# Column-tiled channel sums in a one-core Mamba block: LayerNorm's mean and variance in three column tiles, x_proj in two

## The chip, the cores and the metric

The kernel runs on one core of a Trainium2 chip. The metric is the device time of one execution in microseconds. A core has a matrix engine (TensorE: PE for its products, PEld for its weight loads), a vector engine (VectorE, DVE), an activation engine (ScalarE, ACT), GpSimd (POOL), and a queue engine (SyncE, SP) that mostly issues DMAs. Each engine works through its own instructions in order; semaphores hold an instruction until its inputs are there.

## The reference

The input x has shape (8, 384, 32, 32): 8 images, 384 channels, 1024 tokens. Two layers are computed, each with a residual. The second is a mixture of four experts over the channels. The first is a Mamba block, and the change touches two places in it: the mean and variance over the channels of every token, and the small projection x_proj.

```python
x = x + _L0_conv_ref(_gn(x), ...)      # group norm, then the Mamba block
x = x + _L1_conv_ref(_gn(x), ...)      # group norm, then 4 experts

def _L0_conv_ref(x, ...):
    t = x.transpose(0, 2, 3, 1).reshape(b, L, c)
    mu = t.mean(-1, keepdims=True)
    var = t.var(-1, keepdims=True)
    t = (t - mu) * jax.lax.rsqrt(var + 1e-05) * ln_w + ln_b
    xz = t @ in_proj_w.T
    xm, z = jnp.split(xz, 2, axis=-1)
    xc = ...                             # causal convolution of 3 taps over xm, then silu
    dbc = xc @ x_proj_w.T                # 768 -> 24 + 16 + 16
    dt, Bm, Cm = jnp.split(dbc, [dt_rank, dt_rank + d_state], axis=-1)
    dt = jax.nn.softplus(dt @ dt_proj_w.T + dt_proj_b)
    ...                                  # scan over the tokens with 16 states per channel
    y = (ys + xc * D) * jax.nn.silu(z)
    t = y @ out_proj_w.T
    t = gelu(t @ mlp_w1.T + mlp_b1) @ mlp_w2.T + mlp_b2
    return t
```

## The kernel before

All data are f32. The tokens are cut into NCH = 16 chunks of T = 512 tokens, two per image. Channels lie on the 128 partitions, J = 3 to a partition; the 768 inner channels make ND = 6 blocks of 128 partitions. A product of 128 x 128 weights with 128 x 512 data fills one bank of PSUM.

The middle of the program is a loop of 384 rounds (line 922), 24 per chunk: one round is one block d of channels with one quarter s of the 16 states. In each round GpSimd forms the drive of the scan (L742), ScalarE the decays by exponentials (da_A and da_B, L734), VectorE runs four scans (L750) and half of the read-out (L754, the other half is GpSimd's), and in the round after, TensorE adds the states up by four products of 32 columns each, which stand side by side in the array (y, L776). Everything else is a list of tasks that is fed into the gaps of these rounds: the next chunk's normalization, in_proj, convolution, gate and x_proj; this chunk's dt; the previous chunk's out_proj and MLP; the gate and hidden layer of the experts. These are called fillers here. The second layer of the experts (L1026) is a stage of its own after the loop.

The order is written by a planner when the program is built. The program has three slots per round. A task is a generator that yields the engine it needs next, what it charges for it, and how many slots it wants to wait first. Each slot gives TensorE's account 2.7 (PE_SLOT, line 35), with at most 4 kept over; "bank" means TensorE and a free one of the four shared PSUM banks; a task is resumed where the account allows it, in order of rank and of time. plan(i, k) begins the tasks of round k of chunk i: the convolutions of the next chunk at k = 5 to 10, x_proj at k = 11, norm of the chunk after the next at k = 21, and, in every second chunk, the statistics of the next image at k = 3. The compiler doesn't reorder what the planner wrote (the block is under manual_schedule), and each engine follows it in order.

norm(i) (L257) takes a chunk's mean mu over the 384 channels with three full products into one bank (L265, weights mean_w: the mean over channels already scaled by the group norm), and VectorE subtracts it (L267). ScalarE squares the three parts (L274), with two buffers for them, and three full products sum the squares (L278, var). Then follow a logarithm and an exponential on ScalarE (L280, L281), VectorE's scaling (L283) and ScalarE's weight and bias (L287). All columns of the weights cmean and mean_w are equal, so that every partition of mu and var gets the sum. x_proj(i) (L350) is six products with 56 columns that accumulate in one bank (L358), and a copy by ScalarE into dbc (L363).

One place already works with column tiles: scores(b) forms the gate's logits with three products of 32 columns side by side (L573), copies the 96 partitions (L577, ScalarE), and adds the parts with small products (L580).

## Time and profile before

| what | us |
|---|---|
| median of 3 runs (4087.91 to 4099.21) | 4095.63 |
| the profiled execution | 4110.87 |
| its span, first to last instruction | 4109.0 |
| TensorE busy (share of the span) | 3709.2 (90%) |
| VectorE busy | 3032.3 (74%) |
| GpSimd busy | 2782.5 (68%) |
| ScalarE busy | 2422.7 (59%) |
| products of mu, L265: records, busy | 96, 49.3 |
| products of var, L278: records, busy | 96, 56.8 |
| products of x_proj, L358: records, busy | 192, 91.8 |

An f32 product is run in two passes and leaves two records, so 96 records are 48 products: three in each of 16 chunks. The busy time of a group is the union of its records; the end of a product is modelled, and products overlap in the record, so that the distance from one start to the next says more than a duration. Idle time named after a group of instructions is that of its engine just before them, with the instruction that ended it. The granted clock of TensorE was 0.948 of full speed over the span.

### The profile page before, as it was taken

How to read it: one execution, taken by the hardware profiler on the slowest of the kernel's cores; microseconds unless marked ns; L12 is line 12 of the kernel's file. 1: busy time of each engine (PE TensorE's matmuls, PEld its weight loads, DVE VectorE, ACT ScalarE, POOL GpSimd, SP SyncE). 2: the span in 40 equal slices, each digit the busy share in tenths (PEclk: the TensorE clock that was granted, in tenths of full speed). 3: DMA queues.
4: the chain of work that ended last, by engine and by line, in shares of the span. 5: the costliest groups of instructions: out<-in, count | busy, mean ns of one | idle time of the engine just before them, and what ended most of it. 6: DMA issues, size and time to landing. Idle time of an engine off the chain costs nothing. (4 is left out here: it accounts for less than half of the span.)

```text
span 4109.0 us, 35186 instructions
## 1 busy us (share of the span) xinstructions
PE 3709.2 (90%) x10294; PEld 1385.4 (34%) x10294; DVE 3032.3 (74%) x3081; ACT 2422.7 (59%) x3762; POOL 2782.5 (68%) x1070
## 2 busy tenths in 40 slices
PE   6678888999999999998999989898999899889999
PEld 2123223333333333333333333333333334334444
DVE  4888888878887878888878787878787781165552
ACT  4657676767686768676766677677767663200000
POOL 3898988788877888888878888888878881000000
PEclk8779898999999999999999999999999999899999
DMA  4444444464545454555455444555554543465552
GB/s 127 134 137 134 152 142 158 143 201 164 172 150 180 164 167 151 192 166 175 154 187 172 159 163 159 181 167 166 165 167 155 163 161 96 169 222 189 185 188 98
DMA packets 372499, 665.31 MB, mean 162 GB/s; under 512 B 40252, under 2 KB 151228, under 8 KB 370132
## 3 DMA queue, kind: packets, MB, share of 16 engines
q1 hardware_dynamic: 342352, 610.02, 45.8%
q10 hardware_dynamic: 29956, 53.05, 3.4%
q8 instruction: 83, 1.36, 0.1%
q14 instruction: 108, 0.88, 0.1%
HBM read 535.90 MB, written 127.01 MB: 161 GB/s over the span
## 5 line engine op out<-in xcount | busy, mean ns | idle before, releaser
L742 POOL TENSOR_TENSOR du<-dxr,b 128x2048 f32<-128x2048 f32 x384 | 1740.9, 4534 | 25.1 <-PE y L776 15.1
L754 POOL TENSOR_TENSOR du<-du,c 128x1024 f32<-128x1024 f32 x384 | 905.8, 2359 | 229.2 <-DVE du L750 199.7
L734 ACT ACTIVATE da_A<-dtr_a,w_a_log 128x512 f32<-128x512 f32 x768 | 527.6, 687 | 280.3 <-DVE du L754 122.1
L734 ACT ACTIVATE da_B<-dtr_b,w_a_log 128x512 f32<-128x512 f32 x768 | 527.3, 687 | 260.4 <-DVE du L750 207.2
L478 PE MATMUL hid<-tt,mlp_w 128*128 128x512 f32 x1152 | 541.5, 613 | 63.8 <-ACT h L482 46.7
L776 PE MATMUL y<-du,sel 128*32 128x512 f32 x3072 | 466.3, 642 | 134.1 <-DVE du L754 92.2
L750 DVE TENSOR_TENSOR_SCAN du<-da_B,carry,du 128x512 f32<-128x512 f32 x384 | 488.4, 1272 | 123.2 <-ACT da_B L734 114.8
L619 PE MATMUL e_hid<-xn,e_w 128*128 128x512 f32 x1080 | 519.2, 627 | 55.4 <-ACT r L623 37.9
L295 PE MATMUL g_in<-xt,in_proj 128*128 128x512 f32 x1152 | 554.7, 619 | 13.8 <-ACT xt L287 7.0
L517 PE MATMUL acc<-h,mlp_w 128*128 128x512 f32 x1152 | 543.4, 614 | 24.5 <-ACT h L493 15.9
L750 DVE TENSOR_TENSOR_SCAN du<-da_B,du 128x512 f32<-128x512 f32 x384 | 464.7, 1210 | 130.5 <-ACT da_B L734 114.0
L1026 PE MATMUL acc<-r,w_e_w 128*128 128x512 f32 x1152 | 496.6, 594 | 13.1 <-DVE r L1023 13.1
L750 DVE TENSOR_TENSOR_SCAN da_A<-da_A,carry,du 128x512 f32<-128x512 f32 x384 | 489.3, 1274 | 9.6 <-ACT da_A L734 9.0
L750 DVE TENSOR_TENSOR_SCAN da_A<-da_A,du 128x512 f32<-128x512 f32 x384 | 465.5, 1212 | 27.0 <-ACT da_A L734 25.0
L754 DVE TENSOR_TENSOR du<-da_A,c 128x1024 f32<-128x1024 f32 x384 | 470.3, 1225 | 13.2
L478 PEld LDWEIGHTS hid<-tt,mlp_w 128*128 128x128 f32 x1152 | 215.8, 193 | 366.5 <-issue 239.1
L517 PEld LDWEIGHTS acc<-h,mlp_w 128*128 128x128 f32 x1152 | 216.6, 195 | 343.9 <-issue 247.7
L295 PEld LDWEIGHTS g_in<-xt,in_proj 128*128 128x128 f32 x1152 | 210.0, 194 | 353.5 <-issue 255.1
L619 PEld LDWEIGHTS e_hid<-xn,e_w 128*128 128x128 f32 x1080 | 207.4, 199 | 356.2 <-issue 250.3
L1026 PEld LDWEIGHTS acc<-r,w_e_w 128*128 128x128 f32 x1152 | 219.6, 191 | 290.1 <-issue 287.3
L456 PE MATMUL g_out<-xc,out_proj 128*128 128x512 f32 x576 | 284.0, 641 | 32.9 <-DVE xc L783 32.9
L407 POOL TENSOR_TENSOR dtx<-dt,xc 128x512 f32<-128x512 f32 x96 | 122.1, 1272 | 217.5 <-DVE dt L404 217.5
(129 smaller groups left out, 3030.2 us busy)
## 6 DMA issues: line engine op xcount, KB each, us to landing
dxr<-dxr_dram SPq DMA_DIRECT2D x384, 256.0 KB, 4.7
mlp_w<-in_mlp_w SPq DMA_DIRECT2D x384, 192.0 KB, 2.9
dtr_b<-dtr_dram SPq DMA_DIRECT2D x192, 256.0 KB, 4.2
dtr_a<-dtr_dram SPq DMA_DIRECT2D x192, 256.0 KB, 3.2
r_dram<-r ACTq DMA_DIRECT2D x192, 256.0 KB, 3.5
r<-r_dram SPq DMA_DIRECT2D x64, 768.0 KB, 4.8
in_proj<-in_in_proj SPq DMA_DIRECT2D x192, 192.0 KB, 4.0
e_w<-in_e_w SPq DMA_DIRECT2D x192, 192.0 KB, 3.2
```

The costliest lines, as they stand in the source:

```text
L295: PE.matmul(g, lhsT=w[:, j, :], rhs=xt[i][:, j, :], start=(j == 0), stop=(j == J - 1))
L407: G.tensor_tensor(dtx, dt, xc[i, d], ALU.mult)
L456: PE.matmul(g, lhsT=w[:, d, :], rhs=xc[i, 3 * k + d], start=(k + d == 0), stop=(k == 1 and d == 2))
L478: PE.matmul(g, lhsT=w[:, j, :], rhs=tt[i][:, j, :], start=(j == 0), stop=(j == J - 1))
L517: PE.matmul(g, lhsT=w[:, n, :], rhs=hs[mine[n]], start=(k + n == 0), stop=(k == 1 and n == 2))
L619: PE.matmul(h, lhsT=w[:, j, :], rhs=xn[:, j, :], start=(j == 0), stop=(j == J - 1))
L734: S.activation(out, dtr[i, d][pair][:, j % 2, :], AF.Exp, scale=neg_a[:, d, j, s:s + 1])
L742: G.tensor_tensor(du[r], dxr[i, d], wide(bt[i, s].unsqueeze(1), [P, Q, T]), ALU.mult)
L750: V.tensor_tensor_scan(a if j < 2 else b, a, b, start, ALU.mult, ALU.add)
L754: engine.tensor_tensor(du[r][:, js, :], h, wide(ct[i, s].unsqueeze(1), [P, 2, T]), ALU.mult)
L776: PE.matmul(y[j * m:(j + 1) * m, :], lhsT=sel, rhs=h[:, j, :], start=False, stop=(s == NG - 1), tile_position=(0, j * m), skip_group_check ...
L1026: PE.matmul(acc[j], lhsT=e2[:, e, d, j, :], rhs=r[:, d, :], start=(e + d == 0), stop=(e + d == E + J - 2))
```

## The change

The mean, the variance and x_proj each get a new form. over_channels computes three products of 32 columns, side by side in the array, each into its own 32 partitions of the bank; ScalarE copies these 96 partitions into a buffer, and one full product with the constant matrix spread (1/32 everywhere) adds the three parts and writes the sum to all 128 partitions. x_proj takes its six blocks in three pairs: two products of 64 columns stand side by side, blocks 0, 2 and 4 accumulate in the lower half of the bank, 1, 3 and 5 in the upper half; ScalarE copies the bank, and one product with sum_x adds the halves. Its weights are padded to 64 columns for this, in a zeroed tile. The pool of the square buffers grows from two to three and also holds the copies, the loads of the statistics (which had a buffer of their own) and the skip matrix, which is used once. The planner's charges for these tasks change, and norm begins at k = 18.

```diff
--- before.py
+++ after.py
@@ -126,8 +126,8 @@
 
     wp, p1, p2 = pool("wp", 1), pool("p1", 1), pool("p2", 2)
     pxt, pdu, px1 = pool("pxt", NH), pool("pdu", 3), pool("px1", 2)
-    psq, pz, pxc, ph = pool("psq", 2), pool("pz", ND), pool("pxc", 2 * ND), pool("ph", HID)
-    pbc, pst, pxn, pr = pool("pbc", NG), pool("pst", 1), pool("pxn", 1), pool("pr", 2)
+    psq, pz, pxc, ph = pool("psq", 3), pool("pz", ND), pool("pxc", 2 * ND), pool("ph", HID)
+    pbc, pxn, pr = pool("pbc", NG), pool("pxn", 1), pool("pr", 2)
     pw_in, pw_out, pw_1, pw_2 = pool("pw_in", 3), pool("pw_out", 3), pool("pw_1", 3), pool("pw_2", 3)
     pw_e = pool("pw_e", 3)
     ps_a, ps_b, ps_y = pool("ps_a", 1, space=PSUM), pool("ps_b", 1, space=PSUM), pool("ps_y", 1, space=PSUM)
@@ -153,7 +153,12 @@
     ln_b = weight("ln_b", [P, J])
     conv_w = weight("conv_w", [P, ND, 3])
     conv_b = weight("conv_b", [P, ND])
-    w_x = weight("x_proj", [P, ND, DTR + 2 * NS])
+
+    w_x = wp.tile([P, ND, 64], F32, name="w_x_proj")
+    G.memset(w_x, 0.0)
+    S.dma_start(w_x[:, :, 0:DTR + 2 * NS], io["x_proj"])
+    sum_x = wp.tile([P, DTR + 2 * NS], F32, name="sum_x")
+    V.tensor_tensor(sum_x, ident[:, 0:DTR + 2 * NS], ident[:, 64:64 + DTR + 2 * NS], ALU.add)
     w_dt = weight("dt_proj", [DTR, DI])
     b_dt = weight("dt_b", [P, ND])
     neg_a = weight("a_log", [P, ND, Q, NG])
@@ -166,6 +171,9 @@
     S.dma_start(gate_w[:, :, 0:E], io["gate_w"])
     sum_j = wp.tile([32 * J, E], F32, name="sum_j")
     V.tensor_reduce(sum_j, ident[0:32 * J, 0:32 * J].rearrange("p (j m) -> p m j", j=J)[:, 0:E, :], AX.X, ALU.add)
+
+    spread = wp.tile([32 * J, P], F32, name="spread_j")
+    G.memset(spread, 1.0 / 32)
     e_b1 = weight("e_b1", [P, E * J])
     S.activation(neg_a, neg_a, AF.Exp)
     V.tensor_scalar(neg_a, neg_a, -1.0, None, ALU.mult)
@@ -177,8 +185,6 @@
 
     sel = wp.tile([P, P // Q], F32, name="sel")
     V.tensor_reduce(sel, ident.rearrange("p (m k) -> p m k", k=Q), AX.X, ALU.add)
-    skip = wp.tile([P, P], F32, name="skip")
-    V.tensor_scalar(skip, ident, d_skip[:, 0:1], None, ALU.mult)
 
     edge0 = wp.tile([P, ND, 2], F32, name="edge0")
     V.tensor_copy(edge0, wide(conv_b.unsqueeze(2), [P, ND, 2]))
@@ -236,7 +242,7 @@
                     part = xt[k][:, j, :]
                 else:
                     yield "-", 0, 3
-                    part = pst.tile([P, T], F32, name="part")
+                    part = psq.tile([P, T], F32, name="sq")
                     nc.sync.dma_start(part, chunk_of(io["x"], b * NH + k)[:, j, :])
                     yield "-", 0, 3
                 yield "DVE", 0.7, 0
@@ -248,34 +254,41 @@
         small = bank("shift")
         PE.matmul(small[:, 0:1], lhsT=cmean, rhs=g[:, 1:2], start=True, stop=True)
         yield "ACT", 0.6, 2
-        mean_w = p1.tile([P, P], F32, name="mean_w")
-        S.activation(mean_w, cmean, AF.Identity, scale=g[:, 0:1])
+        mean_w = p1.tile([P, 32], F32, name="mean_w")
+        S.activation(mean_w, cmean[:, 0:32], AF.Identity, scale=g[:, 0:1])
         S.activation(g[:, 1:2], small[:, 0:1], AF.Identity, bias=g[:, 1:2], scale=-float(J))
         free()
         gn[b] = g, mean_w
 
+    def over_channels(out, weights, parts):
+        for j in range(J):
+            PE.matmul(out[32 * j:32 * (j + 1), :], lhsT=weights, rhs=parts[j], start=True, stop=True,
+                      tile_position=(0, 32 * j))
+        yield "ACT", 0.6, 2
+        rows = psq.tile([P, T], F32, name="sq")[0:32 * J, :]
+        S.copy(rows, out[0:32 * J, :])
+        yield "PE", 1, 2
+        PE.matmul(out, lhsT=spread, rhs=rows, start=True, stop=True)
+
     def norm(i):
         while i // NH not in gn:
             yield "-", 0, 1
         g, mean_w = gn[i // NH]
         x = xt[i]
-        yield "bank", 3, 0
+        yield "bank", 1.2, 0
         mu = bank("mu")
-        for j in range(J):
-            PE.matmul(mu, lhsT=mean_w, rhs=x[:, j, :], start=(j == 0), stop=(j == J - 1))
+        yield from over_channels(mu, mean_w, [x[:, j, :] for j in range(J)])
         yield "DVE", 1.8, 2
         V.scalar_tensor_tensor(x, x, g[:, 0:1], wide(mu.unsqueeze(1), [P, J, T]), ALU.mult, ALU.subtract)
         free()
-        sq, var = [], None
-        for j in range(J + 1):
-            if j < J:
-                yield "ACT", 0.65, 2 * (j == 0)
-                sq.append(psq.tile([P, T], F32, name="sq"))
-                S.activation(sq[j], x[:, j, :], AF.Square, bias=g[:, 1:2])
-            if j > 0:
-                yield "PE" if var else "bank", 1, 1
-                var = var or bank("var")
-                PE.matmul(var, lhsT=cmean, rhs=sq[j - 1], start=(j == 1), stop=(j == J))
+        sq = []
+        for j in range(J):
+            yield "ACT", 0.65, 2 * (j == 0)
+            sq.append(psq.tile([P, T], F32, name="sq"))
+            S.activation(sq[j], x[:, j, :], AF.Square, bias=g[:, 1:2])
+        yield "bank", 1.2, 2
+        var = bank("var")
+        yield from over_channels(var, cmean[:, 0:32], sq)
         yield "ACT", 1.2, 2
         S.activation(var, var, AF.Ln, bias=eps)
         S.activation(var, var, AF.Exp, scale=-0.5)
@@ -348,14 +361,21 @@
         exp_ln_tables()
 
     def x_proj(i):
-        g = None
         m = DTR + 2 * NS
-        for d in range(ND):
-            while (i, d) not in xc:
+        for d in range(0, ND, 2):
+            while (i, d) not in xc or (i, d + 1) not in xc:
                 yield "-", 0, 1
-            yield "bank" if d == 0 else "PE", 1, 1 if d % 3 == 0 else 0
-            g = bank("g_x") if d == 0 else g
-            PE.matmul(g[0:m, :], lhsT=w_x[:, d, :], rhs=xc[i, d], start=(d == 0), stop=(d == ND - 1))
+            yield "bank" if d == 0 else "PE", 1.1, 1 if d != 2 else 0
+            if d == 0:
+                g = bank("g_x")
+            for k in range(2):
+                PE.matmul(g[64 * k:64 * (k + 1), :], lhsT=w_x[:, d + k, :], rhs=xc[i, d + k], start=(d == 0),
+                          stop=(d == ND - 2), tile_position=(0, 64 * k))
+        yield "ACT", 0.6, 2
+        halves = psq.tile([P, T], F32, name="sq")
+        S.copy(halves, g)
+        yield "PE", 1, 2
+        PE.matmul(g[0:m, :], lhsT=sum_x, rhs=halves, start=True, stop=True)
         yield "ACT", 0.6, 2
         while i > 0 and (i - 1, ND - 1) not in projected:
             yield "-", 0, 1
@@ -764,6 +784,8 @@
 
         y = yp[i, d] = ps_y.tile([P, T], F32, name="y")
         if i + d == 0:
+            skip = psq.tile([P, T], F32, name="sq")[:, 0:P]
+            V.tensor_scalar(skip, ident, d_skip[:, 0:1], None, ALU.mult)
             PE.matmul(y, lhsT=skip, rhs=xc[i, d], start=True, stop=True)
         else:
             S.activation(y, xc[i, d], AF.Identity, scale=d_skip[:, d:d + 1])
@@ -850,7 +872,7 @@
                 load_c(n, k - (per - NG) - 1)
         if k == 0 and i > 0:
             load_c(i, NG - 1)
-        if k == 21 and n + 1 < NCH:
+        if k == 18 and n + 1 < NCH:
             begin(norm(n + 1))
         if k == 3 and i + NH < NCH:
             begin(next_x(i))
```

## The prediction

> **What bounds the kernel now.** I read the page's busy shares first, then busy time by stretch, then groups by shape, then TensorE's timeline in single rounds, then the waits. Busy time by stretch (length; busy us and instruction count of PE, PEld, DVE, ACT, POOL; granted clock; DMA):
>
> ```profile
> 1000.00:2000.00 1000.00, 926.78 (x2710) 339.90 (x2709) 811.70 (x808) 710.72 (x1111) 824.06 (x314) 0.97 0.52 169
> 3600.00:4109.00 509.00, 496.61 (x1152) 219.59 (x1152) 268.32 (x304) 0.00 (x0) 0.00 (x0) 0.99 0.51 174
> ```
>
> In the scan loop (76 to about 3400 us) TensorE is 93% busy, VectorE 81%, GpSimd 82%, ScalarE 71%. TensorE is the first limit, but not by much. The closing stage holds no LayerNorm and no x_proj, so it stays as it is.
>
> TensorE's timeline over a few rounds gives the prices (start, duration, instruction; each f32 product leaves two records):
>
> ```profile
> 1944.97 1.12 PE L396 MATMUL g_dt<-dbc,w_dt_proj 24*128 24x512 f32 x2
> 1946.02 5.42 PE L456 MATMUL g_out<-xc,out_proj 128*128 128x512 f32 x12
> 1951.37 1.06 PE L776 MATMUL y<-du,sel 128*32 128x512 f32 x8
> 1952.37 2.84 PE L456 MATMUL g_out<-xc,out_proj 128*128 128x512 f32 x6
> ...
> 2140.44 3.06 PE L278 MATMUL var<-sq,cmean 128*128 128x512 f32 x6
> 2145.03 1.10 PE L776 MATMUL y<-du,sel 128*32 128x512 f32 x8 [1.53 <-DVE du L754]
> 2146.06 4.56 PE L456 MATMUL g_out<-xc,out_proj 128*128 128x512 f32 x10
> 2155.33 2.08 PE L456 MATMUL g_out<-xc,out_proj 128*128 128x512 f32 x2 [4.71 <-DVE xc L783]
> ```
>
> Starts count, not the modelled ends. Six products in a train take 1951.37 - 1946.02 = 5.35 us, **0.89 us** each; a group of four 32-column products takes 1952.37 - 1951.37 = **1.00 us**; a product alone between others (g_dt) **1.05 us**. The last four lines show a chunk border: the last round has only the three products of var, and TensorE then waits 1.53 and 4.71 us for VectorE.
>
> The waits between 1000 and 3000 us (waiting instruction, releaser: us, times, longest):
>
> ```profile
> DVE du L750 <- ACT da_B L734: 150.1, 145, 3.2
> DVE xc L314 <- ACT edge L312: 40.2, 20, 2.8
> DVE xc L314 <- ACT xc L308: 26.4, 20, 2.6
> ```
>
> VectorE in turn waits for ScalarE, most of all for the exponentials (da_B).
>
> The same stretch form, cut at the starts of y (chunk 8 is even, chunk 9 odd; the edges are rounds 0 to 21 and 22 to 23 of chunk 8, then 0 to 15, 16 to 22, 23 of chunk 9, and round 0 of chunk 10):
>
> ```profile
> 1723.80:1924.30 200.50, 185.83 (x530) 68.64 (x530) 161.81 (x176) 141.94 (x217) 165.51 (x74) 0.97 0.54 175
> 1924.30:1935.50 11.20, 8.30 (x31) 2.51 (x32) 11.10 (x14) 5.32 (x8) 10.36 (x6) 1.00 0.66 199
> 1935.50:2076.00 140.50, 129.59 (x400) 47.28 (x403) 118.26 (x109) 108.90 (x178) 118.54 (x38) 0.99 0.47 158
> 2076.00:2139.40 63.40, 61.46 (x175) 22.90 (x174) 47.07 (x43) 42.71 (x63) 48.09 (x17) 0.97 0.53 171
> 2139.40:2145.00 5.60, 4.11 (x15) 1.13 (x14) 5.57 (x6) 3.55 (x6) 5.17 (x3) 1.00 0.81 198
> 2145.00:2157.30 12.30, 7.56 (x20) 2.51 (x20) 9.77 (x11) 8.42 (x13) 9.39 (x5) 0.84 0.92 306
> ```
>
> The long stretches are TensorE's (93, 92 and 97%); the ends of chunks are VectorE's (11.10 of 11.20, 5.57 of 5.60). So a product removed in the long stretches gains time, one removed at the end of a chunk gains none.
>
> **What the Trainium skill says.** "TensorEngine Tiling (Array Packing)", Key Properties: tiles run in parallel, and changing the tiling mode drains the engine. The trace agrees in kind: the group of four takes 1.00 us instead of 4 x 0.89, about 0.1 over one product. "TensorE: Matmul & The Clock Gate", Measured speedup vs the span model, gives 2.38 times for three column tiles; the trace shows such triples only in L573, below. The same page, in "Architectural detail: the array is 16× 32×32, not 1× 128×128", has ScalarE's and VectorE's queues strictly in order, with only TensorE's weight loads pulled ahead. The waits agree: VectorE's order ends 92.2 of the 134.1 us that y's products wait in the whole run. So a late copy on ScalarE stops the product that reads it and all TensorE work behind.
>
> **The change part by part.** Groups by shape (busy, mean ns | idle before):
>
> ```profile
> L358 PE MATMUL g_x<-xc,w_x_proj 128*56 128x512 f32 x192 | 91.8, 611 | 4.2 <-ACT xc L346 4.2
> L278 PE MATMUL var<-sq,cmean 128*128 128x512 f32 x96 | 56.8, 719 | 12.0 <-ACT sq L274 12.0
> L573 PE MATMUL g_logits<-x,w_gate_w 128*32 128x512 f32 x96 | 24.0, 745 | 20.5 <-DVE dt L404 17.7 <-ACT x L569 2.7
> L580 PE MATMUL g_logits<-sum_j,x 96*128 96x4 f32 x128 | 17.0, 256 | 0.7 <-ACT x L577 0.7
> L577 ACT COPY x<-g_logits 96x512 f32<-96x512 f32 x16 | 9.1, 572 | 2.0 <-PE g_logits L573 2.0
> ```
>
> 1. *mu and var.* Each loses three products in a train (2.68 us) and gets one triple and one full product. The triple isn't shown in this place: at best it is one product, 0.89; at worst L573's 24.0 / 16 = 1.5, which includes a clock lowered by waiting. I take the group of four's 1.00. The adding product: 0.89 to 1.05; I take 1.05. Gain 0.63 each.
> 2. *x_proj.* Six products (5.35) become three pairs and one product. Pairs of 64 columns occur nowhere: 0.89 to 1.5, or, if they don't overlap, 1.78, which would undo the gain. I take 1.00. Gain 5.35 - 4.05 = 1.3.
> 3. So 2.56 us of TensorE per chunk. 15 chunks do this inside the loop (chunk 0's own is ahead of it): 38 us. Bounds from the ends above: 1.5 + 1.05 for mu and var is a gain of 0.1 each, with x_proj at 5.55 a loss of 0.2, together nothing; at 0.89 throughout one product is saved for mu, one for var and two for x_proj, 3.56 us a chunk, 53 us.
> 4. *Copies.* Three per chunk on ScalarE, 0.57 each from L577: 1.7 us per chunk on an engine that is 71% busy, hidden as long as the adding product stands far enough behind. In L573/L577/L580 the kernel has this very pattern, with L580 stopping TensorE for 0.7 us in 16 chunks. Against it, var waited 12.0 us for squares. Bounds per added wait: 0 to 0.75 (12.0 / 16).
> 5. *Buffers.* The third square buffer ends the squares' wait for var's products (10.3 us over the run), mostly beside other work: nothing. Loads of the statistics now rotate through the same three buffers; each buffer comes round two allocations later, longer than its reader needs, so SP's queue and the weight loads behind gain no wait; if one came, it would cost a DMA landing, 3.9 us.
> 6. *Set-up.* x_proj's weights are zeroed and loaded later, but first needed at 49.97 us; the small tiles fill idle time of POOL and VectorE. Before the loop the chain is serial: mu takes 5.2 us now for three slow products, then one triple, copy and product, -0.7; var +1.0; x_proj +1.8 (copy 0.57, product 1.05, handover). Net +2.1.
> 7. *Placement.* The order of both programs can be listed before either runs, and this decides most. The planner charges less for the tiles, so other products move forward. Filler products per round in a repeating pair of chunks (triple or pair as 1): even chunk, rounds 0 to 21: 174, then 173; rounds 22 to 23: 6, then 1. Odd chunk, rounds 0 to 15: 120, then 117; 16 to 22: 59, then 53; round 23: 3, then 10. So the even chunk loses its products where VectorE sets the time and gains about nothing. The odd chunk loses 9 x 0.89 = 8.0 us in TensorE's stretches, and gets 7 in round 23, 6.2 us, where 1.53 + 4.71 us of waiting stand free. Together -0.9 - 8.0, and +2.0 for ten groups at 0.11 over a product and six lone products at 0.16: -6.9 per pair.
> 8. *What comes back.* Six added waits per pair at 0.15: +0.9. The normalization of even chunks' successors ends later, so convolutions come two to a round in rounds 7 and 8 of odd chunks; VectorE's waits for their ScalarE part average (40.2 + 26.4) / 40 = 1.7 us, and I take part of one, +1.2 (bounds: 0, where the second stands ready meanwhile, and two waits, 3.4). Net -4.8 per pair.
>
> Chunks 3 to 14 are six pairs: -29. Chunks 0 to 2 aren't limited by TensorE (144 fillers in chunk 2 become 138, one of them outside its last two rounds): -1. Chunk 15 and all products after the loop stand as before: 0. With the set-up -28 us: 4110.9 (span 4109.0 plus 1.9 around it) becomes 4083, a ratio of 0.9932. The median of the runs shown lies 0.37% below the profiled execution; by the same ratio it becomes 4095.6 x 0.9932 = 4068.
>
> **The rivals.**
> *A, the whole gain:* neither waits nor convolutions cost anything and pairs overlap fully; 6 x -8.9 is -53, 4043. For it: 61.46 of 63.40 in rounds 16 to 22. Against it: VectorE is 74% busy there, and evens follow. 15%.
> *B, next limits:* rounds of 7 fillers take 7.25 us, and VectorE and GpSimd need about 7 (811.70 and 824.06 per 1000 us, 8.6 us per round); the freed time turns into waits between them, or the 64-column pairs run one after the other. -5, 4090. 20%.
> *C, slower:* the copies stand in ScalarE's order between exponentials of the scan and evictions, exactly where VectorE already waits 150.1 us for da_B. TensorE stops at the adding product, and the scan behind it. 45 such products in the loop; against a best gain of 53 this decides from 1.2 us each, against my sum from 0.15 + 28 / 45 = 0.77. At 1.3 us instead of 0.15: +52 - 28, 4119. For it: before hid TensorE waits up to 2.8 us for ScalarE's evictions (ACT h). Against it: L580's 0.7. 17%.
> *The forecast:* 48%, from 4050 to 4085.
>
> **How the numbers follow.** A measurement here tells 0.3%, 12 us, from no change. Faster: A, 43 of the forecast's 48, 6 of B: 64%. Same: 5, 12 of B, 2 of C: 19%. Slower: 2 of B, 15 of C: 17%. The range runs from beyond A's middle, 4037, to 4110, leaving out most of C.
>
> **What would show it.** Right: mu, var and g_x fall from 49.3, 56.8 and 91.8 busy us to some 33, 33 and 65; odd chunks get shorter and even ones hardly; the 4.71 us wait for xc goes at odd ends and grows at even ones. Wrong: adding products with more than 0.6 us idle before them, g_x near 102 (six products at 0.89 and one at 1.05 in 16 chunks), or VectorE's waits for da_B grown by tens of us.

## The result, and the profile after

The changed kernel takes 4114.54 us (median of 7 runs, 4108.00 to 4121.48) where the kernel before takes 4097.01 us in runs beside it. The ratio is **1.0043, 95% interval 1.0028 to 1.0058**: slower by 17.5 us, where 28 us less were forecast. The profiled execution took 4114.54 us, 3.7 us more than that of the kernel before (4110.87), which was longer than any of the seven runs behind that kernel's median (4087.91 to 4108.82). So the two traces show where time moved, and the medians how much was lost.

The page's head and the busy time by stretch of the changed kernel (length; busy us and instruction count of PE, PEld, DVE, ACT, POOL; granted clock; DMA share, GB/s):

```profile
span 4112.8 us, 35416 instructions
PE 3686.0 (90%) x10390; PEld 1371.7 (33%) x10390; DVE 3030.5 (74%) x3082; ACT 2445.4 (59%) x3810; POOL 2782.4 (68%) x1072
```

```profile
1000.00:2000.00 1000.00, 915.57 (x2724) 332.94 (x2724) 808.17 (x804) 716.15 (x1120) 823.83 (x314) 0.95 0.51 169
```

TensorE is busy for 23 us less (3709.2 before). Between 1000 and 2000 us it is 92% busy instead of 93%, at a granted clock of 0.95 instead of 0.97. The engine became emptier and the loop no shorter.

The groups of the three sums, by shape (busy, mean ns of one | idle of TensorE just before):

```profile
L372 PE MATMUL g_x<-xc,w_x_proj 128*64 128x512 f32 x192 | 61.3, 626 | 6.4 <-ACT xc L359 4.9 <-ACT xc L332 1.2
L271 PE MATMUL mu<-sq,spread_j 96*128 96x512 f32 x32 | 20.2, 717 | 0.8 <-ACT sq L269 0.8
L265 PE MATMUL mu<-xt,mean_w 128*32 128x512 f32 x96 | 20.0, 653 | 0.0
L265 PE MATMUL var<-sq,cmean 128*32 128x512 f32 x96 | 19.9, 628 | 3.5 <-ACT sq L288 3.5
L271 PE MATMUL var<-sq,spread_j 96*128 96x512 f32 x32 | 18.2, 650 | 0.7 <-ACT sq L269 0.7
L378 PE MATMUL g_x<-sq,sum_x 128*56 128x512 f32 x32 | 17.8, 639 | 0.9 <-ACT sq L376 0.8
```

Their sum is 157.4 us; mu, var and g_x took 197.9 before. So 40.5 us of products are saved, where 16 x 2.56 = 41 were forecast. The products that add the parts kept TensorE waiting for their copies 0.8 + 0.7 + 0.9 = 2.4 us in all.

Where the time went is read from the stretches of one pair of chunks, cut as in the prediction: rounds 0 to 21 and 22 to 23 of chunk 8, 0 to 15, 16 to 22 and 23 of chunk 9, round 0 of chunk 10:

```profile
1734.10:1927.20 193.10, 184.93 (x539) 67.80 (x538) 153.09 (x167) 139.66 (x215) 156.74 (x70) 0.97 0.51 168
1927.20:1938.30 11.10, 4.66 (x21) 1.04 (x20) 10.99 (x14) 3.92 (x6) 10.94 (x6) 0.87 0.71 232
1938.30:2078.80 140.50, 128.91 (x398) 47.28 (x398) 120.28 (x111) 111.36 (x182) 120.43 (x39) 0.95 0.47 156
2078.80:2140.10 61.30, 56.32 (x171) 20.65 (x170) 46.08 (x42) 41.51 (x62) 45.98 (x16) 0.97 0.45 152
2140.10:2157.40 17.30, 12.77 (x29) 4.50 (x28) 12.96 (x13) 8.67 (x14) 13.56 (x5) 0.80 0.90 296
2157.40:2163.70 6.30, 6.30 (x21) 2.35 (x20) 5.14 (x5) 4.85 (x8) 4.54 (x1) 1.00 0.85 261
```

Against the lengths before (200.5, 11.2, 140.5, 63.4, 5.6, 12.3): rounds 16 to 22 of the odd chunk lose 2.1 us, rounds 0 to 15 nothing, and **round 23 grows from 5.6 to 17.3**. Round 0, which held the wait of 4.71 us for xc, falls from 12.3 to 6.3. The two together go from 17.9 to 23.6. Of the 7.4 us by which the even chunk's first 22 rounds are shorter, about 5 are that same round 0. The other pairs of chunks 4 to 13 look alike: on average round 23 of the odd chunk goes from 5.5 to 16.9 us and the round 0 after it from 12.1 to 6.3.

TensorE's timeline over that border of chunks (start, duration, instruction; two records to a product). Ahead of it stand the start of round 0 of chunk 9 and two places that show prices:

```profile
1938.38 3.00 PE L798 MATMUL y<-du,sel 128*32 128x512 f32 x8 [4.19 <-DVE du L774]
...
2064.08 1.94 PE L372 MATMUL g_x<-xc,w_x_proj 128*64 128x512 f32 x8
2065.95 5.42 PE L537 MATMUL acc<-h,mlp_w 128*128 128x512 f32 x12
...
2133.80 1.03 PE L265 MATMUL var<-sq,cmean 128*32 128x512 f32 x6
2134.76 5.42 PE L639 MATMUL e_hid<-xn,e_w 128*128 128x512 f32 x12
2140.11 1.06 PE L798 MATMUL y<-du,sel 128*32 128x512 f32 x8
2141.11 2.84 PE L639 MATMUL e_hid<-xn,e_w 128*128 128x512 f32 x6
2143.78 1.02 PE L271 MATMUL var<-sq,spread_j 96*128 96x512 f32 x2
2145.03 2.84 PE L639 MATMUL e_hid<-xn,e_w 128*128 128x512 f32 x6 [0.22 <-DMA e_w<-in_e_w]
2152.18 5.31 PE L639 MATMUL e_hid<-xn,e_w 128*128 128x512 f32 x6 [4.30 <-DMA e_w<-in_e_w]
2157.42 1.07 PE L798 MATMUL y<-du,sel 128*32 128x512 f32 x8
```

Two 64-column pairs take 2065.95 - 2064.08 = 1.87 us, 0.94 each; the triple at 2133.80 takes 0.96. Round 23 now holds the products that the forecast put into free waiting, and most of them are the experts' hidden layer. The last three wait 4.30 us for their weights and then take 2157.42 - 2152.18 = 5.24 us instead of the 2.67 that such three take at 2141.11. The delay reaches the others: VectorE waits 2.09 us and GpSimd 1.83 us for the y of 2157.42.

The end of the even chunk, from which the new order took five of six products, has its price too. TensorE there waits 4.19 us for VectorE's read-out, and the group y after it takes 2.94 us to the next start (1941.32) instead of 1.00. On average over these pairs round 0 of the odd chunk goes from 8.5 to 10.1 us.

Why the weights are late stands in SP's queue of DMA issues (start, duration of the issue):

```profile
2140.79 0.38 SPq L223 DMA_DIRECT2D e_w<-in_e_w  x1
2141.26 0.88 SPq L391 DMA_DIRECT2D b<-bc_dram  x1
2142.24 0.59 SPq L391 DMA_DIRECT2D c<-bc_dram  x1
2142.92 1.66 SPq L408 DMA_DIRECT2D dtr_a<-dtr_dram  x2
2144.68 3.53 SPq L408 DMA_DIRECT2D dtr_b<-dtr_dram  x2
2148.31 0.54 SPq L223 DMA_DIRECT2D e_w<-in_e_w  x1
```

The load stands behind those of the next chunk's scan and is issued at 2148.31; TensorE goes on 3.9 us later. Busy time in steps of 4 us over the same border (columns as in the stretches above):

```profile
2144.00:2148.00 4.00, 3.65 (x8) 1.06 (x6) 3.97 (x4) 0.69 (x1) 3.47 (x3) 1.00 1.01 330
2148.00:2152.00 4.00, 0.00 (x0) 0.00 (x0) 1.18 (x2) 1.99 (x3) 3.66 (x1) 0.80 0.98 347
2152.00:2156.00 4.00, 3.82 (x5) 1.79 (x6) 3.49 (x4) 2.54 (x4) 1.77 (x2) 0.50 0.85 265
```

The DMA engines are full (1.01, 0.98), TensorE stands for the whole middle step, and in the last one it is granted half its clock.

The waits between 1000 and 3000 us (waiting instruction, releaser: us, times, longest), before:

```profile
PE g_out L456 <- DVE xc L783: 20.2, 6, 4.7
PE e_hid L619 <- ACT r L623: 19.0, 10, 2.1
PE y L776 <- DVE du L754: 18.4, 20, 1.9
PE e_hid L619 <- DMA e_w<-in_e_w: 0.4, 1, 0.4
```

and after:

```profile
DVE du L770 <- ACT da_B L754: 156.9, 157, 3.9
...
PE y L798 <- DVE du L774: 28.1, 10, 4.2
PE e_hid L639 <- ACT r L643: 26.9, 9, 4.9
...
DVE xc L805 <- PE y L798: 23.2, 14, 2.5
PE hid L498 <- ACT da_A L754: 22.9, 5, 5.2
PE e_hid L639 <- DMA e_w<-in_e_w: 19.9, 9, 4.7
...
PE g_out L476 <- DVE xc L805: 2.7, 4, 1.6
```

VectorE waits hardly longer for the exponentials than before (150.1), so the trace doesn't show the copies disturbing the scan. TensorE's wait for xc is nearly gone (20.2 before), but others are new or longer: for the experts' weights, for VectorE at the ends of the even chunks (y behind du), for ScalarE in the middle of the odd chunks (hid behind da_A, five times in these 2000 us, 5.2 us at most), and for ScalarE's evictions r. VectorE in turn waits 23.2 us for y, 5.0 before. TensorE's idle time in this stretch is 173 us, 150 before.

### The profile page after: what moved, and what is told of

Its sections match the earlier page's. It is cut to its first block, busy times and chain, and to the rows that moved or that the text cites. A ratio compares the mean times of both kernels' runs of the same rounds, so it can differ in the third digit from the quotient of the medians.

```text
span 4112.8 us, 35416 instructions
## 1 busy us (share of the span) xinstructions
PE 3686.0 (90%) x10390; PEld 1371.7 (33%) x10390; DVE 3030.5 (74%) x3082; ACT 2445.4 (59%) x3810; POOL 2782.4 (68%) x1072
## 5 line engine op out<-in xcount | busy, mean ns | idle before, releaser
L639 PE MATMUL e_hid<-xn,e_w 128*128 128x512 f32 x1080 | 546.1, 655 | 115.7 <-ACT r L643 47.3
L798 PE MATMUL y<-du,sel 128*32 128x512 f32 x3072 | 484.7, 640 | 155.0 <-DVE du L774 96.7
L476 PE MATMUL g_out<-xc,out_proj 128*128 128x512 f32 x576 | 267.8, 614 | 5.5 <-DVE xc L805 5.5
```

The source lines that it names most:

```text
L476: PE.matmul(g, lhsT=w[:, d, :], rhs=xc[i, 3 * k + d], start=(k + d == 0), stop=(k == 1 and d == 2))
L639: PE.matmul(h, lhsT=w[:, j, :], rhs=xn[:, j, :], start=(j == 0), stop=(j == J - 1))
L798: PE.matmul(y[j * m:(j + 1) * m, :], lhsT=sel, rhs=h[:, j, :], start=False, stop=(s == NG - 1), tile_position=(0, j * m), skip_group_check ...
```

## The experiments

The runs are named e1 to e15; the "fifth run" of an expectation is e5. The expectations set three theories against each other. Theory 1, or the weights: the products that moved to the border wait for their weights, and the new order loses what the tiles save (from e5 on: whatever the new order does, it ate the gain). Theory 2, rival C of the prediction: each sum now goes TensorE, ScalarE, TensorE, and these hand-ons cost. Theory 3: other engines hold the rounds in which the freed time lies, so that less work for TensorE gains nothing. A fourth came up on the way: a new order of this program costs by itself, whatever is in it. All ratios are to the kernel before in runs beside them. Where a run below is said to keep an order, the records of TensorE, VectorE, ScalarE and GpSimd in its trace stand in that order throughout the loop, but for the instructions that it changes.

**The order alone, and the weights earlier.** The kernel before with norm at k = 18, nothing else changed (e2):

```diff
-        if k == 21 and n + 1 < NCH:
+        if k == 18 and n + 1 < NCH:
```

> The kernel before with one number changed: norm begins at k = 18 instead of 21. No tiles, no copies. By the order it too gets nine products of experts into round 23 of odd chunks. Theory 1: slower than before by 10 to 30 us, ratio 1.0025 to 1.0075. Theories 2 and 3: as before, 0.998 to 1.002.

4115.02 us, **1.0049 [1.0033, 1.0066]**: one number in the planner costs as much as the whole change, with every product as it was. The time is what theory 1 expected, but its mechanism is nearly absent: between 1000 and 3000 us a product waits for e_w once, 2.8 us.

The changed kernel with the experts' weights loaded one product earlier in SP's list (e1):

```diff
+                w_e.load()
...
-        w_e = Stream(pw_e, [("e_w1", u) for i in range(NCH) for u in range(E * J)])
+        w_e = Stream(pw_e, [("e_w1", u) for i in range(NCH) for u in range(E * J)], late=True)
```

> The changed kernel, with each load of an expert weight tile written one product earlier into SyncE's list; the order on all other engines stays. Theory 1 (products of the experts that the new order puts into round 23 of odd chunks wait for weights whose load stands behind the scan's loads, 4.4 us plus some 2.7 us at a lowered clock, in six pairs of chunks): the wait goes, 25 to 43 us less than the changed kernel's 4114, ratio to before 0.994 to 0.999. Theory 2 (the added copies and products cost the time by their waits) and theory 3 (the freed time is in places where other engines are the limit): as the changed kernel, 1.003 to 1.006.

4158.01 us, 1.0145 [1.0127, 1.0164]. A miss for all three: the wait for e_w goes, and the kernel is some 43 us slower than the changed one, with a mean clock of 0.934 over its span (0.941 in the changed kernel, 0.948 before). Between 1000 and 3000 us SP now stands 401.0 us for products e_hid that free a buffer of weights (166.2 in the changed kernel), and ScalarE waits 82.5 us for the scan's dtr_a (46.1). So the load that was put forward holds back the scan's loads behind it, and this run doesn't tell what the weights' wait alone costs.

The changed kernel with norm at k = 20, charged as for full products and with shorter waits between the steps, so that no expert product lies in round 23 (e4):

```diff
-        yield "bank", 1.2, 0
+        yield "bank", 3, 0
...
-        if k == 18 and n + 1 < NCH:
+        if k == 20 and n + 1 < NCH:
```

> All the tiles, copies and adding products of the changed kernel, but with the planner charged as for full products (3 for the first, nothing for the adding one), shorter waits in slots, and norm at k = 20; by the order no product of an expert stands in round 23. Theory 1: faster than before, 20 to 40 us, ratio 0.990 to 0.995. Theory 2: slower, 1.003 or more, since the adding products stand closer behind their copies. Theory 3: 0.999 to 1.002.

4115.52 us, 1.0045 [1.0027, 1.0063]. Another miss for the weights as the only cause: without expert products at that border, and with no wait for e_w between 1000 and 3000 us, nothing is gained. Other waits are long instead (y for VectorE 34.6 us, hid for h 43.1).

**x_proj alone, by two column tiles, copy and adding product** (e3), LayerNorm as before:

```diff
+                PE.matmul(g[64 * k:64 * (k + 1), :], lhsT=w_x[:, d + k, :], rhs=xc[i, d + k], start=(d == 0),
+                          stop=(d == ND - 2), tile_position=(0, 64 * k))
+        yield "ACT", 0.6, 2
+        halves = psq.tile([P, T], F32, name="sq")
+        S.copy(halves, g)
+        yield "PE", 1, 2
+        PE.matmul(g[0:m, :], lhsT=sum_x, rhs=halves, start=True, stop=True)
```

> x_proj by two column tiles alone; LayerNorm and its start at k = 21 as before. The order has three products of experts in round 23 of odd chunks. Theory 1: the saved 1.3 us in each of 15 chunks shows for the most part, 10 to 20 us less, ratio 0.995 to 0.9975. Theory 2: a third of the added waits, 1.000 to 1.002. Theory 3: 0.999 to 1.001.

4106.02 us, 1.0021 [1.0012, 1.0029]: the part of the change that was to save 1.3 us of TensorE per chunk costs 9 us by itself, in the order that its steps bring.

**Work and order taken apart.** The old order, with 4 of the 12 products of each chunk left out (one of mu, one of var, two of x_proj; e5):

```diff
-        for j in range(J):
-            PE.matmul(mu, lhsT=mean_w, rhs=x[:, j, :], start=(j == 0), stop=(j == J - 1))
+        for j in range(J - 1):
+            PE.matmul(mu, lhsT=mean_w, rhs=x[:, j, :], start=(j == 0), stop=(j == J - 2))
...
+                if j != 2:
...
+            if d not in (1, 4):
```

> The kernel before with four of its twelve products for mu, var and x_proj left out in every chunk (one each of mu and var, two of x_proj; the result of that part changes), everything else in its old order, no copies. It takes 4 x 0.89 = 3.6 us of TensorE from each of 15 chunks, 53 us. Theory 1 (the work is worth its time, and the new order ate the gain): 30 to 50 us less than before, ratio 0.988 to 0.9925. Theory 2 (the copies and their waits ate it): the same. Theory 3 (where these products stand other engines hold the round, so that less work for TensorE only lengthens its waits): at most 10 us, 0.9975 to 1.000.

4066.03 us, **0.9922 [0.9910, 0.9933]**. In the loop 15 x 4 x 0.89 = 53 us of products are gone and 32 us of time: where the order stays, a microsecond of TensorE is worth 0.6. Theory 3 expected at most 10 us.

The new order (the steps and charges of the changed norm and x_proj, norm at k = 18) with full products and no copies (e7):

```diff
+    def over_channels(out, weights, parts):
+        for j in range(J):
+            PE.matmul(out, lhsT=weights, rhs=parts[j], start=(j == 0), stop=(j == J - 1))
+        yield "ACT", 0.6, 2
+        yield "PE", 1, 2
```

> The changed kernel's planner steps, with the full products of before in the places of the tiles and no copies or adding products: the new order with the old work, 38 us more of TensorE than the changed kernel. Theory 1: 4135 to 4150, ratio to before 1.009 to 1.013. Theory 2: below the changed kernel, 0.999 to 1.003. Theory 3: as the changed kernel, 1.003 to 1.006.

4118.32 us, **1.0048 [1.0036, 1.0060]**. So the order of the changed kernel costs 20 us (22 by the medians), and the tiles in it give 4 back, or nothing within the intervals. The run also has the change's third square buffer and its shared loads of the statistics, but e2 pays as much for an order without them. Theory 1 expected 4135 to 4150. Its waits between 1000 and 3000 us include the two that the kernel before lacks or hardly has:

```profile
PE hid L491 <- ACT da_A L747: 22.0, 5, 5.2
PE e_hid L632 <- DMA e_w<-in_e_w: 16.5, 5, 4.2
```

These sit in the order, not in the tiles or copies.

The changed kernel without copies and adding products (a fourth strip of columns is filled in their place; e8):

```diff
-        rows = psq.tile([P, T], F32, name="sq")[0:32 * J, :]
-        S.copy(rows, out[0:32 * J, :])
         yield "PE", 1, 2
-        PE.matmul(out, lhsT=spread, rhs=rows, start=True, stop=True)
```

> The changed kernel without the copies and the adding products, in its order; the sums stay in parts (the normalization and x_proj are not computed to the end; a fourth strip is filled by one more 32-column product). 3 x 1.05 us less of TensorE and 1.7 us less of ScalarE per chunk than the changed kernel, and no waits for copies. Theory 1: some 20 us below the changed kernel, 0.998 to 1.002. Theory 2: 40 us or more below it, under 0.996. Theory 3: 1.002 to 1.005.

4094.17 us, 0.9994 [0.9988, 1.0001]. 45 adding products of 1.05, 47 us of TensorE, and 45 copies are gone, and 20 us of time. Against e7 it saves 38 + 47 = 85 us of products and 24 us of time: 0.3 each, half of what the old order gives, and unevenly, 4 for the first 38 and 20 for the other 47.

**The chain in the old order.** Tiles, copies and adding products where the last full products stood, copy and product one slot (a third of a round) apart and not charged (e6):

```diff
+        yield "-", 0, 1
+        rows = psq.tile([P, T], F32, name="sq")[0:32 * J, :]
+        S.copy(rows, out[0:32 * J, :])
+        yield "-", 0, 1
+        PE.matmul(out, lhsT=spread, rhs=rows, start=True, stop=True)
```

> The tiles, copies and adding products, but with the planner charged and timed exactly as before (norm at k = 21, the copies and adding products uncharged in slots that the old steps waited through), so that all other instructions keep their old order. Theory 1: 15 to 38 us less than before, 0.991 to 0.9965. Theory 2: not faster, 1.000 to 1.006. Theory 3: 0.998 to 1.001.

4122.20 us, 1.0063 [1.0050, 1.0077]: where e5 gained by less work in the old order, the tiles with their copies lose. Who waits, 1000 to 3000 us:

```profile
DVE xt L282 <- PE mu L271: 20.5, 10, 3.2
ACT dbc L386 <- PE g_x L381: 20.1, 6, 4.1
...
PE var L271 <- ACT sq L269: 15.1, 9, 3.8
```

This is rival C's mechanism: the adding product of var waits 1.7 us for its copy, VectorE 2 us for the mean, ScalarE 3.4 us for x_proj. Together with e7: given room between its steps the chain doesn't wait, but the room makes a new order; in the old order it waits.

**Other orders, and the weights taken out altogether.** The kernel before with norm at k = 22 (e11):

```diff
-        if k == 21 and n + 1 < NCH:
+        if k == 22 and n + 1 < NCH:
```

> The kernel before with norm at k = 22 instead of 21: nearly the old order, no product of an expert in round 23. If only the wait for weights makes an order dear: as before, 0.9985 to 1.0015. If any order that departs from the old one costs time by other waits: 1.002 to 1.006.

4122.69 us, 1.0062 [1.0050, 1.0074], with no expert product in round 23. A move by one round later costs as much as three rounds earlier, through other waits (y's products wait 34.3 us for VectorE between 1000 and 3000 us, up to 6.3; 18.4 before).

The experts' loads removed from the loop, every hidden product reading one resident tile of weights, in the kernel before (e9), the changed one (e10) and the full products in the new order (e13):

```diff
+        w = pw_e.tile([P, 3, P], F32, name="e_w1", tag="w")
+        nc.sync.dma_start(w, io["e_w1"][0])
...
-                w = w_e.take("e_w1", u)
```

> The kernel before with all hidden products of the experts reading one weight tile, loaded once (their result changes; all other work and the order stay). For the difference to the next run. Some gain from fewer transfers under both theories, 0.990 to 1.000.

> The changed kernel with the same simplification, so that no product of an expert can wait for weights in round 23. The changed kernel stands 17 us above the one before. If the wait for weights at the ends of odd chunks (4.4 us and the slow clock after it, some 6 us in six pairs) makes the new order dear, this run gains 25 to 38 us more than the run before it does and ends 8 to 20 us below it. If the order costs its time elsewhere, it stays 10 to 20 us above it.

> The seventh run (new order, full products, no copies) with one resident weight tile for the experts' hidden products, as in the tenth. If the weights' wait took what the tiles saved, the tenth run is now 20 to 35 us below this one, which ends at 1.003 to 1.007. If the new order's other waits and the slow clock after them take it, this run is within 8 us of the tenth, 0.997 to 1.000.

| order and products | with loads | one resident tile |
|---|---|---|
| before | 1 | 0.9984 [0.9974, 0.9993] (4091.47) |
| changed | 1.0043 [1.0028, 1.0058] | 0.9984 [0.9973, 0.9996] (4093.97) |
| full products, new order | 1.0048 [1.0036, 1.0060] | 1.0062 [1.0046, 1.0078] (4124.49) |

Without the loads the changed kernel is as fast as the one before; e10 ends between its two forecasts. But the same edit gives nothing to the full products in the same order, where the wait for e_w was nearly as long (16.5 against 19.9). With the loads away the tiles are worth some 30 us (1.0062 to 0.9984), most of what their work is; with them, 4. By this e13 ends where theory 1 put it.

Two things in the traces speak against reading this as the price of the wait at the border. First, much of what the edit gives lies behind the loop, where the change does nothing. From the end of the last scan to the end of the program the traces take 703.2 us before, 703.0 in the changed kernel and 700.4 in e7; with one resident tile 688.3, 689.6 and 686.9. The last hidden products, in the changed kernel and in e10:

```profile
3557.53 8.37 PE L639 MATMUL e_hid<-xn,e_w 128*128 128x512 f32 x12 [12.26 <-ACT r L643]
3541.64 5.42 PE L640 MATMUL e_hid<-xn,e_w 128*128 128x512 f32 x12 [1.98 <-ACT r L644]
```

What is left for the loop, an estimate from the ratios less these 13 to 15 us, has no one sign: some 11 us less in the changed kernel, 8 more in the kernel before and 19 more with full products in the new order. Second, the border itself. In e10 round 23 of chunk 9 and round 0 of chunk 10 are these:

```profile
2134.50:2144.30 9.80, 9.80 (x29) 3.87 (x28) 8.10 (x8) 5.41 (x9) 9.27 (x3) 1.00 0.82 293
2144.30:2153.80 9.50, 6.69 (x21) 2.27 (x20) 8.83 (x9) 6.57 (x12) 7.98 (x4) 1.00 0.95 326
```

Round 23 takes 9.8 us instead of 17.3 and has no wait, but round 0 takes 9.5 instead of 6.3 and the rounds after it more too: over chunks 4 to 13 a pair takes 425.3 us, as in the changed kernel (425.4).

The last pair asks the same of e8, whose wait for e_w is the longest. The first (e14) is e8 once more, with all loads; the second (e15) has one resident tile:

> The eighth run once more (changed kernel without copies and adding products), beside the thirteenth on one chip, as the base of the fifteenth: 0.998 to 1.001.

> The eighth run (changed kernel without copies and adding products) with one resident weight tile. If the weights' wait held back what TensorE is spared, 30 us or more below the eighth, 0.992 or less. If not, at most 10 us, 0.996 to 0.999.

4092.22 us, 0.9988 [0.9981, 0.9996], and 4090.92 us, 0.9987 [0.9979, 0.9996]: no gain, though behind the loop e15 too takes 13.5 us less. The wait at the border, with all loads:

```profile
PE e_hid L633 <- DMA e_w<-in_e_w: 27.2, 10, 5.3
```

and with one tile:

```profile
PE y L793 <- ACT y L786: 32.4, 15, 6.3
```

Where the wait for the weights is gone, one for ScalarE's start value of y has grown by nearly as much (11.1 us with all loads); it grows in e10 (11.6 to 20.8) and e13 (11.5 to 29.9) as well. So with its weights there, TensorE waits for something else soon after the border. Why the sum is so uneven (0.16% gained in the kernel before, 0.59% in the changed one, 0.14% lost with full products in the new order, less than the intervals can tell, and 0.01% gained here) stays open.

**A version that beats both** (e12). x_proj by three pairs in the old order, LayerNorm as before, and no adding product: ScalarE's copy of the lower half into dbc stays where it was, and VectorE adds the upper half from the bank. The change's third square buffer and shared loads of the statistics are in it too.

```diff
         S.copy(dbc[i], g[0:m, :])
+        yield "DVE", 0.75, 1
+        V.tensor_tensor(dbc[i], g[64:64 + m, :], dbc[i], ALU.add)
         free()
```

> x_proj by three pairs of 64-column products with the planner's old steps, and no adding product: ScalarE copies the lower half as it did the whole, and VectorE adds the upper half from PSUM. LayerNorm as before, so the order of everything else is the old one. TensorE is spared 5.35 - 3.0 = 2.35 us in 15 chunks, 35 us, VectorE gets 0.7 us each, 10 us. If work removed in the old order counts by 0.6 as in the fifth run: 10 to 25 us less, 0.994 to 0.9975. If any further handover in this chain costs what it saves: 0.999 to 1.003.

**4081.73 us, 0.9957 [0.9940, 0.9973]**, 18 us faster than the kernel before. Its groups (busy, mean ns | idle before):

```profile
L359 PE MATMUL g_x<-xc,w_x_proj 128*64 128x512 f32 x192 | 52.6, 611 | 3.3 <-ACT xc L345 2.1 <-ACT xc L318 1.2
...
L367 DVE TENSOR_TENSOR dbc<-g_x,dbc 56x512 f32<-56x512 f32 x16 | 11.1, 693 | 3.1 <-ACT dbc L365 2.6
```

39 us of TensorE are saved (91.8 before) for 11 us of VectorE, and the mean clock between 1000 and 3000 us stays at 0.97. The mean time of a pair of chunks (4 to 13) falls from 423.8 to 417.5 us, but the trace is of the fastest of six executions (4065.91) and that of the kernel before of a long one (4110.87), so this overstates the 18 us of the medians. What the third buffer gives was not tried alone; it can end ScalarE's waits for one, 3.9 us in these 2000 us before. e3 differs from e12 in the adding product and in the order that its steps bring, which no run separates; the two are 24 us apart.

## Why the prediction was wrong

The forecast was 4068 us, faster by 28; the kernel is slower by 17.5 and lies just above the range. It gave 17% to a slower kernel, nearly all to rival C, whose mechanism does not show in this kernel. None of its signs of being wrong came either (adding products with over 0.6 us of idle time, g_x near 102, da_B's waits up by tens of us): the loss came by a way that it had not listed. Its busy shares (93, 81, 82 and 71%) are those of 1000 to 2000 us; over 76 to 3400 us TensorE was 90% busy (2994.14 of 3324.00). By its steps:

1. *mu and var* and 2. *x_proj*: right. From start to next start, where no wait follows, triples took 0.96 to 0.99 us for the 1.00 taken, pairs of 64 columns 0.94 in a row and 1.01 alone for 1.00, and the adding products 0.86 (var), 0.95 (mu) and 1.00 (x_proj) for 1.05. By busy time the adding products stand at 1.26, 1.14 and 1.11 (20.2, 18.2 and 17.8 by 16) and g_x at 79.1 instead of 65, since busy time includes stretches of half clock, in which a pair took up to 2.15 us; at the same count e12's pairs need 52.6.
3. *2.56 us per chunk*: right in sum, 40.5 us of busy time for 41.
4. *Copies*: right. 0.57 to 0.58 us each, and 2.4 us of waiting in all, 0.05 per adding product for the 0.15 taken. Rival C's sign didn't appear in this kernel; e6 shows that it would have, had the chain been fitted into the old order.
5. *Buffers*: right as far as the trace shows: var's idle time for its squares fell from 12.0 to 3.5 us, and the loads of the statistics let VectorE wait 1.9 us between 1000 and 3000 us, 3.5 before. What the third buffer is worth alone was not measured. 6. *Set-up*: 2.7 us later (first scan at 78.70 instead of 76.00) for 2.1.
7. **Placement: this step failed.** It counted TensorE's products in each round, priced the moves by them, and came to a gain of 6.9 us per pair of chunks. With the old work in the new order, e7, the moves cost 20 to 22 us in all. For one, it took round 23 of odd chunks for room that "stands free". Free was TensorE, not the way there. Nine of the ten products there are now the experts', each three with weights of their own, and those loads stand in SP's queue behind the scan's when the DMA engines are full. The border took 23.6 us instead of 17.9, so that seven more products cost 5.7 us where they were priced at nothing; 4.30 us of waiting and 2.6 us of halved clock are in it. e10 shows that the weights alone don't explain it: with them there, the border takes 9.8 + 9.5 = 19.3 us, and the rounds after it lose what it gains. The prediction had listed SP's queue, but only for the loads of the statistics (step 5). The same step priced the stretches by TensorE's share alone: rounds 16 to 22 should have lost 5.3 us and lost 2.1, with a new wait of 4.93 us for an eviction r in them; rounds 0 to 15 should have lost 2.7 and lost none, with hid now waiting up to 5.2 us behind da_A, and with the half clock after the 4.19 us at the emptied end of the even chunk, which the prediction took to cost nothing. There it expected the wait for xc to grow; y's wait for the read-out grew. The direction was right for the odd chunks: over chunks 4 to 13, from VectorE's first scan of one chunk to that of the next, odd chunks went from 210.5 to 208.8 us and even ones, into which the border's wait falls by this count, from 213.3 to 216.6. The pair went from 423.8 to 425.4, +1.6 instead of -4.8, and that against a trace of the kernel before that is 14 us longer than its median.
8. *What comes back*: too small, and the wrong item. No cost of the convolutions shows (VectorE's two waits there fell from 66.6 to 53.2 us). What came back is TensorE's own: between 1000 and 3000 us its idle time grew by 23 us, about the 24 that the tiles free there (2000 / 424 pairs of 2 x 2.56), and it ran slower. The time lost to the clock, added up over its busy stretches as one minus the clock granted in each, is 57.5 us before and 71.8 after. But e8 and its repeat e14 differ by 8 in this sum (83.0 and 74.6), and e4 and e7, as slow as the changed kernel, lose only 58.8 and 61.4. So the clock takes part in this kernel's loss and isn't what makes an order dear.

Behind both lies one thing the forecast didn't price: an order. e7 says it directly: +22 us for the new order and, as the rest to the measured 17.5, -4 for the tiles in it. The forecast priced the order at about nothing: -4.8 us per pair, against 2 x 2.56 of saved work. e2 and e11 show that this order isn't specially bad: norm begun three rounds earlier or one later costs the unchanged work 20 to 25 us. The waits and the half clock above show where this order loses time; why the old order is better than all the others tried here stays open.

Shown: the cost of the order, the worth of removed work in the old order (e5) and the smaller worth in the new one, the exposed chain in e6, the border's wait and its half clock. Not settled: how much of the 20 us is the experts' weights, if any. Removing their loads closes the gap between the changed kernel and the one before, and nothing in the two other programs with this order; e2 and e4 are as slow with hardly a wait for them.

## What to carry to other kernels

In a program whose order is planned or written by hand, run the change's order alone, with the old work, and the change's work alone, in the old order, before anything is read into their sum: one start time moved by one to three rounds cost 20 to 25 us here, where 38 us of saved products gave back 4. A stretch where the busiest engine waits is room only for work whose inputs are there, so look at the DMA queue and its share at that place before pricing moved work at nothing. Of several forms that save the same work, try the one that sends nothing back to the busiest engine and keeps the old order: halves added by VectorE as they leave the bank won 18 us, where a copy and a product, in an order of their own, lost 9.

## What the hardware showed that was not expected

A wait can cost TensorE more than its length. After a wait of 4.30 us three products took 5.24 us instead of 2.67, at a granted clock of 0.50. The Trainium skill has the rule ("TensorE: Matmul & The Clock Gate", What's actually happening: after at least one idle window of about 3.4 us the clock is halved). For the long waits the trace agrees: between 1000 and 3000 us all waits above 4 us, 4 before and 17 after, are followed by half clock, in stretches of 3.41 us or a multiple of it. But here shorter waits are followed by it too, as this one of 2.75 us in the kernel before, where three products take 4.24 us to the next start (1806.34):

```profile
1802.10 4.32 PE L478 MATMUL hid<-tt,mlp_w 128*128 128x512 f32 x6 [2.75 <-ACT h L482]
```

Less work does not lower the clock by itself. In the same 2000 us it is 0.97 before, 0.95 after and 0.94 without copies and adding products (e8), but 0.97 in e4, which has all the tiles, and 0.97 in e12.

Pairs of 64 f32 columns do run side by side: a pair takes 0.94 us in a row of two and 1.01 alone, where two full products one after the other take 1.78 (2 x 0.89). That is close to a triple of 32 columns (0.96 to 0.99) and to a group of four (1.00).
